# Head of a pairwise outer-product batch norm: order of loads, of the shift and of the gram terms, and which tiles start from raw products

## The chip, the cores and the metric

The kernel runs on one core of one Trainium2 chip. The metric is the device time of one execution in microseconds (us); lower is better. Times are medians of the fast runs; a profile is one execution. The kernel before takes 1891.19 us (median of 6 runs, 1891.06 to 1891.61), so 1 us is 0.05%, and the runs of one kernel spread over about 0.5 us.

Engines: PE multiplies matrices, DVE is the vector engine, ACT the scalar engine, POOL is GpSimd, SP only issues DMAs.

## The reference, cut to what matters

```python
# xi, xj: (1024, 39, 16) f32, W: (1, 16, 16)
rows, cols = np.tril_indices(39, k=-1)                # 741 pairs
cross  = xj[:, rows, :, None] * xi[:, cols, None, :]  # (1024, 741, 16, 16)
mean   = cross.mean(axis=(0, 2, 3)); var = ((cross - mean) ** 2).mean(axis=(0, 2, 3))
out    = ((cross - mean) * rsqrt(var + 1e-5) * gamma + beta) * W
```

The output has 1024 x 741 x 256 floats, 777 MB. The statistics of all pairs need the whole batch, but they follow from sums over the inputs (6 MB) alone, through small matrix products (the "grams"). Nothing can be stored before they are there, so the kernel has a head without stores and then a long stretch of stores.

## The kernel before

A partition holds eight batch rows, here called samples. Work goes by tiles: one row `r` of the triangle (its `r` pairs) for two samples. Tiles 0 to 3 are row 19. A scaled tile is made in two steps: POOL scales xi by each pair's factor (`scale_xi`), ACT and POOL multiply by xj (`products`), and DVE adds the pair's offset and multiplies by W (`finish`, one instruction for each pair; POOL does 13% of the pairs). The first tiles are made from raw products while the statistics are still under way, and then need an affine step and a weighing.

```python
RAW = 2
...
raw0 = raw_products(0, nc.scalar, range(32))
raw1 = raw_products(1, nc.scalar, range(8))
...                                   # sums of sample 0 of xj and xi together, shift
for n in range(2 * NT // T):          # 8 steps: two samples of xj or of xi
    square(n)                         # ACT
    emit(raw0, 2)                     # ACT, two raw products of tile 0
    moments(n)                        # DVE, the sum of squares
    ...
    if n % 2 == 1:
        gram(n // 2 * T)              # PE, three terms for each of two samples
    if n in (1, 3):
        sums(n + 3, n + 5)            # DVE
        ...
emit(raw_products(1, nc.gpsimd, range(8, 32)), 24)
nc.scalar.copy(w_dve, w_sb)
emit(raw0, 8)
nc.scalar.copy(g1, ps_g[0][0:F, 0 : 2 * F + 1])
...                                   # small operations on 39 x 39 tables
apply(0)                              # table of row 19, all partitions
affine(0)                             # ACT and POOL: y * s + t, pair by pair
weigh(0)                              # DVE: y * W, with the stores
scale_xi(2)
affine(1)
weigh(1)
apply(2)
apply(1)
for n in range(1, len(tiles)):
    if n == 1:
        products(2)
        scale_xi(3)
        continue
    scale_xi(n + 2)
    finish(n)                         # DVE with the stores
    ...
    products(n + 1)
```

## Time and profile before

| | before |
|---|---|
| time | 1891.19 us |
| span of the profiled run | 1889.3 us |
| first store issued | 41.27 us |
| DMA in the long middle (160 to 1800 us) | full, 423 GB/s |
| DVE, ACT, POOL busy | 92%, 86%, 83% |

Read it as two stretches: a head, and a long stretch in which the DMA engines are full. A "hole" below is time between the first store and that long stretch in which the DMA engines have too little to move.

### The profile page before, as it was taken

To read this page: it belongs to the slowest core of one execution; us is meant where nothing else is said; L and a number is where in the kernel's file an instruction comes from. 1 tells how busy PE (TensorE), PEld (TensorE's weight loads), DVE (VectorE), ACT (ScalarE), POOL (GpSimd) and SP (SyncE) were. 2 spreads that over 40 slices of the span, in tenths; PEclk is the share of its full clock that TensorE was granted. 3 is DMA by queue.
4 is the path that set the end of the run, shared out by engine and by line. 5 is a ranking of instruction groups with operands and counts; after the bars stand their busy time and mean duration, and the time that the engine had idled before them with its cause. 6 is when DMAs were issued, how large, how long until landed. Compare 5 with 4: busy or idle time off the path is not lost. (4 is left out here: it accounts for less than half of the span.)

```text
span 1889.3 us, 10288 instructions
## 1 busy us (share of the span) xinstructions
PE 24.5 (1%) x128; PEld 23.1 (1%) x128; DVE 1730.7 (92%) x2612; ACT 1621.3 (86%) x3625; POOL 1574.5 (83%) x1985
## 2 busy tenths in 40 slices
PE   3100000000000000000000000000000000000000
PEld 3100000000000000000000000000000000000000
DVE  7999999998989898989898989899999999999996
ACT  8999989898989898989898989888888888888762
POOL 9798878788888888888888888888888888888972
DMA  4999999999999999999999999999999999999999
GB/s 164 390 418 429 425 427 429 430 424 429 424 425 426 424 424 426 422 425 425 424 425 423 426 423 426 422 422 422 421 421 422 418 415 419 416 419 419 415 419 390
DMA packets 70288, 783.67 MB, mean 415 GB/s; under 512 B 5057, under 2 KB 6209, under 8 KB 15937
## 3 DMA queue, kind: packets, MB, share of 16 engines
q1 hardware_dynamic: 69632, 780.46, 98.3%
q10 hardware_dynamic: 576, 2.56, 0.3%
q14 instruction: 79, 0.64, 0.1%
q8 instruction: 1, 0.02, 0.0%
HBM read 6.00 MB, written 776.99 MB: 414 GB/s over the span
## 5 line engine op out<-in xcount | busy, mean ns | idle before, releaser
L238 DVE SCALAR_TENSOR_TENSOR y_sb<-y_sb,st_sb,w_dve 128x512 f32<-128x512 f32 x2542 | 1678.5, 740 | 131.5 <-issue 128.3
L139 ACT ACTIVATE y_sb<-xs,xj_sb 128x256 f32<-128x256 f32 (+32 forms) x3544 | 1576.4, 539 | 223.5 <-DMA out_dram<-y_sb 171.8
L141 POOL TENSOR_SCALAR y_sb<-xs,xj_sb 128x560 f32<-128x560 f32 (+35 forms) x1256 | 643.2, 536 | 35.1 <-DMA out_dram<-y_sb 32.6
L230 POOL TENSOR_TENSOR y_sb<-y_sb,w_sb 128x1024 f32<-128x1024 f32 (+4 forms) x138 | 442.0, 3203 | 11.5
L159 POOL TENSOR_TENSOR xs<-xi_sb,st_sb 128x576 f32<-128x576 f32 (+37 forms) x150 | 187.8, 1252 | 225.3 <-ACT y_sb L139 217.8
L226 POOL TENSOR_SCALAR y_sb<-y_sb,st_sb 128x512 f32<-128x512 f32 x384 | 259.4, 692 | 12.9 <-ACT y_sb L139 12.9
L204 DVE TENSOR_TENSOR y_sb<-y_sb,w_dve 128x2560 f32<-128x2560 f32 (+5 forms) x8 | 21.0, 2682 | 2.3 <-ACT y_sb L194 2.3
L139 ACT ACTIVATE y_sb<-xi_sb,xj_sb 128x304 f32<-128x304 f32 x40 | 18.7, 534 | 0.1
L414 PE MATMUL ps<-y_sb 39*128 39x38 f32 (+37 forms) x76 | 16.5, 397 | 5.6 <-DVE y_sb L402 5.6
L414 PEld LDWEIGHTS ps<-y_sb 39*128 39x128 f32 x76 | 16.3, 329 | 5.8 <-issue 5.8
L194 ACT ACTIVATE y_sb<-y_sb,st_sb 128x512 f32<-128x512 f32 x20 | 14.2, 797 | 0.0
L196 POOL TENSOR_SCALAR y_sb<-y_sb,st_sb 128x512 f32<-128x512 f32 x18 | 13.5, 771 | 0.3 <-issue 0.3
L141 POOL TENSOR_SCALAR y_sb<-xi_sb,xj_sb 128x304 f32<-128x304 f32 x24 | 11.9, 518 | 0.0
L299 DVE TENSOR_REDUCE y_sb<-y_sb 128x78 f32<-128x1248 f32 x8 | 11.1, 1442 | 0.0
L277 DVE TENSOR_REDUCE y_sb<-xj_sb 128x78 f32<-128x1248 f32 (+1 forms) x5 | 5.9, 1189 | 5.6 <-DMA xj_sb<-in_r_xj_dram 5.6
L293 ACT ACTIVATE y_sb<-y_sb 128x1248 f32<-128x1248 f32 x8 | 9.9, 1243 | 1.3 <-POOL y_sb L283 1.1
L283 POOL TENSOR_TENSOR y_sb<-xj_sb,y_sb 128x1248 f32<-128x1248 f32 x4 | 9.3, 2314 | 1.9 <-ACT y_sb L327 1.9
L283 POOL TENSOR_TENSOR y_sb<-xi_sb,y_sb 128x1248 f32<-128x1248 f32 x4 | 9.3, 2318 | 0.0
L316 PE MATMUL ps<-y_sb 128*39 128x79 f32 x48 | 7.2, 339 | 16.5 <-DVE y_sb L299 16.5
L316 PEld LDWEIGHTS ps<-y_sb 128*39 128x39 f32 x48 | 6.1, 183 | 17.4 <-DVE y_sb L299 9.6
L277 DVE TENSOR_REDUCE y_sb<-xi_sb 128x78 f32<-128x1248 f32 (+1 forms) x5 | 5.9, 1186 | 0.0
L259 POOL TENSOR_SCALAR_AFFINE_SELECT y_sb<-y_sb 39x4992 f32<-39x4992 f32 x1 | 4.6, 4623 | 0.0
(45 smaller groups left out, 16.9 us busy)
## 6 DMA issues: line engine op xcount, KB each, us to landing
out_dram<-y_sb SPq DMA_DIRECT2D x32, 3072.0 KB, 13.7
out_dram<-y_sb SPq DMA_DIRECT2D x28, 2816.0 KB, 15.7
out_dram<-y_sb SPq DMA_DIRECT2D x32, 1664.0 KB, 14.2
out_dram<-y_sb SPq DMA_DIRECT2D x16, 3328.0 KB, 17.2
out_dram<-y_sb SPq DMA_DIRECT2D x30, 1536.0 KB, 15.2
out_dram<-y_sb SPq DMA_DIRECT2D x12, 3840.0 KB, 17.6
out_dram<-y_sb SPq DMA_DIRECT2D x12, 3584.0 KB, 18.1
out_dram<-y_sb SPq DMA_DIRECT2D x22, 1792.0 KB, 17.4
```

What stands on the lines that cost most here:

```text
L139: nc.scalar.activation(y, src, AF.Copy, scale=scale)
L141: engine.tensor_scalar(y, src, scale, 1.0, ALU.mult, ALU.mult)
L159: nc.gpsimd.tensor_tensor(xs, xi_sb[:, t0 : t0 + T, 0:r, :], s_sb[:, :, n0 : n0 + r, :].to_broadcast([P, T, r, E]), ALU.mult,)
L194: nc.scalar.activation(y[:, :, c, :], y[:, :, c, :], AF.Identity, bias=t_c, scale=s_c)
L196: nc.gpsimd.tensor_scalar(y[:, :, c, :], y[:, :, c, :], s_c, t_c, ALU.mult, ALU.add)
L204: nc.vector.tensor_tensor(y[:, :, c0:c1, :], y[:, :, c0:c1, :], w_dve.unsqueeze(1).to_broadcast([P, T, c1 - c0, EE]), ALU.mult,)
L226: nc.gpsimd.tensor_scalar(y[:, :, c, :], y[:, :, c, :], t_sb[:, n0 + c : n0 + c + 1], 1.0, ALU.add, ALU.mult)
L230: nc.gpsimd.tensor_tensor(y[:, :, split:r, :], y[:, :, split:r, :], w_sb.unsqueeze(1).to_broadcast([P, T, r - split, EE]), ALU.mult,)
L238: stt(y[:, :, c, :], y[:, :, c, :], t_sb[:, n0 + c : n0 + c + 1], w_dve.to_broadcast([P, T, EE]), ALU.add, ALU.mult,)
L283: nc.gpsimd.tensor_tensor(devs[n % 7], sources[x][:, t0 : t0 + T], shift[:, x : x + 1, :].unsqueeze(3).to_broadcast([P, T, F, E]), ALU.sub ...
L316: nc.tensor.matmul(acc[0:F, 0 : 2 * F + 1], lhs, fb[:, t], start=t == 0, stop=t == NT - 1)
L414: nc.tensor.matmul(ps[:, :, first[r] - n0 : first[r] - n0 + r], pick[:, r, :], stq[:, :, 0:r], start=True, stop=True,)
```

## The change

The intent is a shorter head: the first sample of xi arrives first and alone, so that its shift is known sooner and POOL can begin; the gram terms are issued as soon as their inputs are there, so that the table operations run beside the last matmuls; only tile 0 is made raw, and tile 1 takes the ordinary route but is finished sample by sample, so that its stores can begin when half of it is there.

```diff
-    (0, 2, 5, 9, 14, 19), (0, 6, 12, 19), ...
+    (0, 2, 5, 9, 14, 19), (0, 4, 9, 14, 19), ...
-POOL_I, POOL_I_LONG = 4, 5
+POOL_I, POOL_I_LONG, POOL_I_FIRST = 4, 5, 6      # tiles 1 and 2: POOL has 6 of 16 products
-LOADS = (0, 1, 2, 4, 8)
+LOADS = (1, 2, 3, 4, 8)
-    RAW = 2
+    RAW = 1
@@ finish
+        size = 1 if n == RAW else T
+        for t in range(0, T, size):
+            for c0, c1 in zip(bounds(n), bounds(n)[1:]):
+                for c in range(c0, min(c1, split)):
+                    stt(y[:, t : t + size, c, :], ...)
+                store(n, c0, c1, t, t + size)
@@ loads
+        nc.sync.dma_start(xi_sb[:, 0, 0 : F // 2], xi_v[:, 0, 0 : F // 2])
+        nc.scalar.dma_start(xi_sb[:, 0, F // 2 : F], xi_v[:, 0, F // 2 : F])
+        nc.sync.dma_start(xj_sb[:, 0], xj_v[:, 0])
@@ statistics: xi first in every step
-            t0, x = n // 2 * T, n % 2
+            return n // 2 * T, 1 - n % 2
+        def gram(n):
+            ...
+                terms = ((0, fa[:, t, 0:F]), (2, ones[:, 0:F])) if x else ((1, fa[:, t, F : 2 * F]),)
             moments(n)
+            gram(n)
-            if n in (1, 3):
-                sums(n + 3, n + 5)
+            if n == 1:
+                sums(4, 8)
@@ tables
-        nc.scalar.activation(p_kk, k, AF.Square)
+        nc.vector.tensor_mul(p_kk, k, k)
...
@@ first tiles
         apply(0)
-        affine(0)
+        apply(1)
+        affine(0, range(0, 11))
+        scale_xi(1)
+        affine(0, range(11, mid))
         weigh(0)
+        products(1)
         scale_xi(2)
-        affine(1)
-        weigh(1)
-        apply(2)
-        apply(1)
```

(Cut: the shift's copies, the order of the small operations, the row groups of the tables; eight raw products of tile 0 that go from ACT to POOL; ACT's first square root, which loads its table and now stands before ACT's last load.)

More of the change, by code (lines that the diff above doesn't have):

```diff
@@ L19 @@
 FIRST_PIECES = (
-    (0, 2, 5, 9, 14, 19), (0, 6, 12, 19), (0, 4, 11, 19), (0, 9, 19), (0, 10, 20), (0, 9, 18), (0, 10, 20), (0, 9, 18)
+    (0, 2, 5, 9, 14, 19), (0, 4, 9, 14, 19), (0, 4, 11, 19), (0, 9, 19), (0, 10, 20), (0, 9, 18), (0, 10, 20), (0, 9, 18)
 )
-POOL_I, POOL_I_LONG = 4, 5
+POOL_I, POOL_I_LONG, POOL_I_FIRST = 4, 5, 6
 POOL_SHARE = 0.13
-LOADS = (0, 1, 2, 4, 8)
+LOADS = (1, 2, 3, 4, 8)
 ROW_GROUPS = (
-    (19, 20, 0, None), (15, 19, 1, None), (20, 25, 1, None), (1, 15, 2, 8), (25, 32, 3, 16), (32, 39, 4, 24)
+    (19, 20, 0, None), (15, 19, 1, None), (20, 25, 2, 1), (1, 15, 2, 8), (25, 32, 3, 16), (32, 39, 4, 24)
 )
@@ L169, in products @@
         xs = xs_of.pop(n)
-        split = E - (POOL_I_LONG if tiles[n][0] > TWO else POOL_I)
+        split = E - (POOL_I_FIRST if n < 3 else POOL_I_LONG if tiles[n][0] > TWO else POOL_I)
         for t in range(T):
@@ L173, in products, with store @@
                 product(n, nc.scalar if i < split else nc.gpsimd, t, i, xs[:, t])
-    def store(n, c0, c1):
+    def store(n, c0, c1, t_from=0, t_to=T):
         r, t0, _ = tiles[n]
         n0 = first[r]
-        step = 1 if r > ONE and c1 == r else T
-        for t in range(0, T, step):
+        step = 1 if r > ONE and c1 == r else t_to - t_from
+        for t in range(t_from, t_to, step):
             nc.sync.dma_start(
@@ L184, in store, with affine @@
             )
-    def affine(n):
+    def affine(n, pairs):
         r = tiles[n][0]
         y = view(n)
-        for c in range(r):
+        for c in pairs:
             s_c = st_sb[:, 0, first[r] + c : first[r] + c + 1]
@@ L235, in finish @@
             )
-        for c0, c1 in zip(bounds(n), bounds(n)[1:]):
-            for c in range(c0, min(c1, split)):
-                stt(
-                    y[:, :, c, :],
-                    y[:, :, c, :],
-                    t_sb[:, n0 + c : n0 + c + 1],
-                    w_dve.to_broadcast([P, T, EE]),
-                    ALU.add,
-                    ALU.mult,
-                )
-            store(n, c0, c1)
+        size = 1 if n == RAW else T
+        for t in range(0, T, size):
+            for c0, c1 in zip(bounds(n), bounds(n)[1:]):
+                for c in range(c0, min(c1, split)):
+                    stt(
+                        y[:, t : t + size, c, :],
+                        y[:, t : t + size, c, :],
+                        t_sb[:, n0 + c : n0 + c + 1],
+                        w_dve.to_broadcast([P, size, EE]),
+                        ALU.add,
+                        ALU.mult,
+                    )
+                store(n, c0, c1, t, t + size)
     with tc.manual_schedule():
+        nc.gpsimd.memset(ones, 1.0)
+        nc.sync.dma_start(xi_sb[:, 0, 0 : F // 2], xi_v[:, 0, 0 : F // 2])
+        nc.scalar.dma_start(xi_sb[:, 0, F // 2 : F], xi_v[:, 0, F // 2 : F])
+        nc.sync.dma_start(xj_sb[:, 0], xj_v[:, 0])
         for t0, t1 in zip(LOADS, LOADS[1:]):
+            if t1 == NT:
+                nc.scalar.activation(shift_r, ones[0:F, 0:1], AF.Sqrt)
             nc.sync.dma_start(xj_sb[:, t0:t1], xj_v[:, t0:t1])
@@ L255, in tile_pair_outer_batchnorm @@
         nc.sync.dma_start(w_sb[:, 0, :], w.rearrange("o i j -> (o i j)").partition_broadcast(P))
-        nc.gpsimd.memset(ones, 1.0)
         nc.gpsimd.memset(fb[:, :, 2 * F : 2 * F + 1], 1.0 / NB)
@@ L273, in part, with sums @@
             return slice(x * F, (x + 1) * F)
-        def sums(t0, t1):
-            for x in range(2):
+        def sums(t0, t1, xs=(1, 0)):
+            for x in xs:
                 nc.vector.tensor_reduce(
@@ L279, in sums, with step_of @@
                 )
+        def step_of(n):
+            return n // 2 * T, 1 - n % 2
         def deviation(n):
-            t0, x = n // 2 * T, n % 2
+            t0, x = step_of(n)
             nc.gpsimd.tensor_tensor(
@@ L290, in square @@
         def square(n):
-            scale = 0.25 / NB**0.5 if n % 2 else 0.25
+            _, x = step_of(n)
+            scale = 0.25 / NB**0.5 if x else 0.25
             nc.scalar.activation(devs[n % 7], devs[n % 7], AF.Square, scale=scale)
         def moments(n):
-            t0, x = n // 2 * T, n % 2
+            t0, x = step_of(n)
             to = fb if x else fa
-            at = slice(F, 2 * F)
-            nc.vector.tensor_reduce(to[:, t0 : t0 + T, at], devs[n % 7], AX.X, ALU.add)
-        def means(n):
-            t0, x = n // 2 * T, n % 2
-            to = fb if x else fa
-            stt(
-                to[:, t0 : t0 + T, 0:F],
-                total[:, t0 : t0 + T, part(x)],
-                1.0 / (E * NB) if x else 1.0 / E,
-                ps_u[:, x : x + 1, :].to_broadcast([P, T, F]),
-                ALU.mult,
-                ALU.subtract,
-            )
@@ L313, in gram, with means @@
-        def gram(t0):
+            nc.vector.tensor_reduce(
+                to[:, t0 : t0 + T, F : 2 * F], devs[n % 7], AX.X, ALU.add
+            )
+        def means(t0, t1):
+            for x, to in enumerate((fa, fb)):
+                stt(
+                    to[:, t0:t1, 0:F],
+                    total[:, t0:t1, part(x)],
+                    1.0 / (E * NB) if x else 1.0 / E,
+                    ps_u[:, x : x + 1, :].to_broadcast([P, t1 - t0, F]),
+                    ALU.mult,
+                    ALU.subtract,
+                )
@@ L314, in gram @@
+        def gram(n):
+            t0, x = step_of(n)
             for t in range(t0, t0 + T):
-                for acc, lhs in zip(ps_g, (fa[:, t, 0:F], fa[:, t, F : 2 * F], ones[:, 0:F])):
+                terms = ((0, fa[:, t, 0:F]), (2, ones[:, 0:F])) if x else ((1, fa[:, t, F : 2 * F]),)
+                for acc, lhs in terms:
                     nc.tensor.matmul(
-                        acc[0:F, 0 : 2 * F + 1], lhs, fb[:, t], start=t == 0, stop=t == NT - 1
+                        ps_g[acc][0:F, 0 : 2 * F + 1], lhs, fb[:, t], start=t == 0, stop=t == NT - 1
@@ L318, in gram @@
                     )
-        raw0 = raw_products(0, nc.scalar, range(32))
-        raw1 = raw_products(1, nc.scalar, range(8))
-        nc.scalar.activation(shift_r, ones[0:F, 0:1], AF.Sqrt)
-        sums(0, 1)
-        nc.tensor.matmul(ps_s[:, 0 : 2 * F], ones, total[:, 0], start=True, stop=True)
-        nc.tensor.matmul(ps_c[0:F, 0:1], total[:, 0, 0:F], ones[:, 0:1], start=True, stop=True)
-        nc.scalar.activation(
-            shift.rearrange("p x f -> p (x f)"), ps_s[:, 0 : 2 * F], AF.Copy, scale=k_s
-        )
+        raw0 = raw_products(0, nc.scalar, range(24))
@@ new lines, in tile_pair_outer_batchnorm @@
+        raw0_pool = raw_products(0, nc.gpsimd, range(24, 32))
+        ps_shift = (ps_g[0][:, 0:F], ps_s[:, 0:F])
+        for x in (1, 0):
+            sums(0, 1, (x,))
+            nc.tensor.matmul(ps_shift[x], ones, total[:, 0, part(x)], start=True, stop=True)
+        nc.tensor.matmul(ps_c[0:F, 0:1], total[:, 0, 0:F], ones[:, 0:1], start=True, stop=True)
+        ps_u = ps_s[:, 2 * F : 4 * F].rearrange("p (x f) -> p x f", x=2)
+        nc.scalar.activation(shift[:, 1], ps_shift[1], AF.Copy, scale=k_s)
@@ L330, in tile_pair_outer_batchnorm @@
+        nc.scalar.activation(ps_u[:, 1], shift[:, 1], AF.Copy, scale=1.0 / NB)
+        nc.scalar.activation(shift[:, 0], ps_shift[0], AF.Copy, scale=k_s)
+        nc.scalar.copy(ps_u[:, 0], shift[:, 0])
         nc.scalar.activation(shift_r, ps_c[0:F, 0:1], AF.Copy, scale=k_s)
-        ps_u = ps_s[:, 2 * F : 4 * F].rearrange("p (x f) -> p x f", x=2)
-        nc.scalar.copy(ps_u[:, 0], shift[:, 0])
-        nc.scalar.activation(ps_u[:, 1], shift[:, 1], AF.Copy, scale=1.0 / NB)
         def cell(n):
@@ L343, in tile_pair_outer_batchnorm @@
         sums(1, 2)
-        means(0)
-        means(1)
-        sums(2, 4)
-        means(2)
-        means(3)
+        means(0, 2)
+        sums(2, 3)
+        sums(3, 4)
+        means(2, 4)
         for n in range(7):
@@ L355, in tile_pair_outer_batchnorm @@
             moments(n)
+            gram(n)
             if n == 0:
                 deviation(7)
-            if n % 2 == 1:
-                gram(n // 2 * T)
-            if n in (1, 3):
-                sums(n + 3, n + 5)
-                means(n + 3)
-                means(n + 4)
-        emit(raw_products(1, nc.gpsimd, range(8, 32)), 24)
+            if n == 1:
+                sums(4, 8)
+                means(4, 8)
+        emit(raw0_pool, 8)
         nc.scalar.copy(w_dve, w_sb)
-        emit(raw0, 8)
         nc.scalar.copy(g1, ps_g[0][0:F, 0 : 2 * F + 1])
+        emit(raw0, 1)
         nc.scalar.copy(e_aa, ps_g[1][0:F, 2 * F : 2 * F + 1])
-        emit(raw0, 5)
+        emit(raw0, 4)
         e_ab, e_abb, e_a = g1[:, 0:F], g1[:, F : 2 * F], g1[:, 2 * F : 2 * F + 1]
@@ L380, in tile_pair_outer_batchnorm @@
         stt(k, p_b, u, e_ab, ALU.mult, ALU.add)
-        stt(q2, e_ab, u, p_aab, ALU.mult, ALU.add)
+        stt(p_q1, p_bb, u, e_abb, ALU.mult, ALU.add)
         stt(k, p_v, e_a, k, ALU.mult, ALU.add)
-        stt(q2, p_v_half, e_aa, q2, ALU.mult, ALU.add)
-        stt(p_q1, p_bb, u, e_abb, ALU.mult, ALU.add)
-        stt(p_q2, q2, 2.0, p_v, ALU.mult, ALU.mult)
         nc.vector.tensor_add(q1, p_q1, e_abb)
         stt(p_mean, p_v, u, k, ALU.mult, ALU.add)
-        nc.scalar.activation(p_kk, k, AF.Square)
+        nc.vector.tensor_mul(p_kk, k, k)
+        stt(q2, e_ab, u, p_aab, ALU.mult, ALU.add)
         stt(q1, q1, u, p_aabb, ALU.mult, ALU.add)
+        stt(q2, p_v_half, e_aa, q2, ALU.mult, ALU.add)
+        nc.vector.tensor_sub(q1, q1, p_kk)
+        stt(p_q2, q2, 2.0, p_v, ALU.mult, ALU.mult)
         nc.vector.tensor_add(q1, q1, p_q2)
-        nc.vector.tensor_sub(q1, q1, p_kk)
         nc.vector.tensor_scalar(p_var, q1, 0.0, BN_EPS, ALU.max, ALU.add)
@@ L396, in tile_pair_outer_batchnorm @@
         nc.scalar.activation(rstd, inv, AF.Sqrt)
-        emit(raw1, 8)
         nc.vector.tensor_mul(p_newton, p_var, rstd)
@@ L429, in tile_pair_outer_batchnorm @@
         apply(0)
-        affine(0)
+        apply(1)
+        affine(0, range(0, 11))
+        scale_xi(1)
+        affine(0, range(11, mid))
         weigh(0)
+        products(1)
         scale_xi(2)
-        affine(1)
-        weigh(1)
-        apply(2)
-        apply(1)
         for n in range(1, len(tiles)):
-            if n == 1:
-                products(2)
-                scale_xi(3)
-                continue
             if n + 2 < len(tiles):
```

## The prediction

> **What bounds the kernel now.** I read the busy table by stretches first, then the order of instructions in the first 90 us, then the list of waits. The split of the span at 41.27 us (the first store is issued), 82 and 160 us gives this; the columns that matter are the DVE, ACT and POOL busy times, then at the end the share of the DMA engines and GB/s.
>
> ```profile
> core 0: us, PE busy (x) PEld busy (x) DVE busy (x) ACT busy (x) POOL busy (x), PEclk, DMA share, GB/s
> 0.00:41.27 41.27, 12.58 (x74) 11.33 (x74) 28.87 (x48) 33.00 (x65) 38.38 (x44) 1.00 0.37 146
> 41.27:82.00 40.73, 11.95 (x56) 11.74 (x56) 39.02 (x41) 40.73 (x84) 32.92 (x46) 1.00 0.91 368
> 82.00:160.00 78.00, 0.00 (x0) 0.00 (x0) 77.97 (x121) 78.00 (x180) 71.19 (x93) 1.00 1.00 420
> 160.00:1800.00 1640.00, 0.00 (x0) 0.00 (x0) 1516.33 (x2301) 1434.03 (x3252) 1387.87 (x1767) 1.00 1.00 423
> ```
>
> From 82 us on the DMA engines are full and stay full: 777 MB must go out at about 423 GB/s, and nothing in the change touches that. What can move is when the stores start and how many holes the DMA has before 82 us. Slices of 1 us show the last hole at 81 to 82 us (share 0.61), larger ones at 70 to 72 us (0.33, 0.00). So up to 82 us the stores wait for the engines, and the end of the kernel moves by as much as the first store of the fourth tile (tile 3) moves. The order of instructions up to there (start, duration, engine, line; x is a count of merged ones):
>
> ```profile
> 4.93 0.80 DVE L277 TENSOR_REDUCE y_sb<-xj_sb 128x39 f32<-128x624 f32 x1 [4.93 <-DMA xj_sb<-in_r_xj_dram]
> 7.63 2.31 POOL L283 TENSOR_TENSOR y_sb<-xj_sb,y_sb 128x1248 f32<-128x1248 f32 x1 [1.93 <-ACT y_sb L327]
> 23.83 5.52 DVE L299 TENSOR_REDUCE y_sb<-y_sb 128x78 f32<-128x1248 f32 x4
> ...
> 31.77 0.20 ACT L372 COPY y_sb<-ps 39x79 f32<-39x79 f32 x1
> 32.00 0.25 DVE L380 SCALAR_TENSOR_TENSOR y_sb<-ps,y_sb 39x39 f32<-39x39 f32 x1 [2.65 <-ACT y_sb L372]
> 36.42 0.19 DVE L402 SCALAR_TENSOR_TENSOR y_sb<-ps,y_sb 39x39 f32<-39x39 f32 x1
> 37.41 0.18 DVE L425 TENSOR_TENSOR ps<-ps,st_sb 128x19 f32<-128x19 f32 x1 [0.80 <-PE ps L414]
> 39.13 14.20 ACT L194 ACTIVATE y_sb<-y_sb,st_sb 128x512 f32<-128x512 f32 x20
> 40.03 1.22 DVE L204 TENSOR_TENSOR y_sb<-y_sb,w_dve 128x1024 f32<-128x1024 f32 x1 [2.13 <-ACT y_sb L194]
> 41.27 45.59 SPq L181 DMA_DIRECT2D out_dram<-y_sb  x13
> 41.44 19.74 DVE L204 TENSOR_TENSOR y_sb<-y_sb,w_dve 128x1536 f32<-128x1536 f32 x7 [0.19 <-ACT y_sb L194]
> 53.23 37.13 ACT L139 ACTIVATE y_sb<-xs,xj_sb 128x304 f32<-128x304 f32 x84
> 63.96 26.42 DVE L238 SCALAR_TENSOR_TENSOR y_sb<-y_sb,st_sb,w_dve 128x512 f32<-128x512 f32 x40 [1.44 <-ACT y_sb L139]
> ```
>
> Three milestones: M, the last sum of squares on DVE ends, 29.35; S, the table of the first row group is ready (37.73 plus 0.17), 37.90; D, DVE begins to finish tile 2, 63.96. From D on DVE runs without a pause, and tile 3's first nine pairs are ready 26 steps of 0.659 us later (17 pairs of tile 2, nine of tile 3), at 81.1: the hole just named. So the gain is the shift of D.
>
> **What the Trainium skill says.** "VectorE: DVE Perf Modes", section on the TRN2 errata: a fixed cost per instruction, not a factor, so halved operands cost more than half. The trace agrees: a 512-element finishing step starts every 0.659 us, and where one waited it resumed in parts of 0.128 and 0.531 (512/0.96 GHz is 0.533). I take 0.128 + 256/960 = 0.395 us for a 256-element step. "DMA: Bandwidth & Descriptors", Queues, rings and completion order: each DMA engine takes turns between the queue rows; so loads of the two queues share the rate[...]. Here xj's and xi's first samples, issued together, landed at 4.91 and 5.07. "ScalarE: Activation LUTs", What ACT_TABLE_LOAD costs: about 1283 ns; the trace has 1.28 at 3.15, hidden behind the loads before and after.
>
> **The change, part by part.**
> *Loads and sums.* xi's first sample alone, half on each queue, is 0.32 MB ahead of the first sum instead of 0.64. At the 0.42 MB/us of the early slices that is 0.76 us; I take the first sum at 4.2 instead of 4.93. But DVE, not POOL, bounds the statistics: it works 23.45 of the 24.47 us from 4.93 to 29.40, while POOL's last deviation ends at 25.87. Its work hardly changes: eight one-sample sums at 0.725, two four-sample sums at 2.66, eight sums of squares at 1.36, six means at 0.15 to 0.23, together 23.0. What changes is its waiting. Sharing the rate as before, I expect about 0.4 us for xj's first sample, 0.3 for samples two and three, 0.3 for the second square, and 0.85 for xi's samples 4 to 7, which landed at 15.99 and would land near 15.1 (0.16 MB fewer on that queue) when DVE is free at 14.25. M = 4.2 + 23.0 + 1.85 = 29.05: 0.3 earlier.
> *M to S.* Before 8.55 us: 2.65 until DVE starts (six terms on PE, then ACT's copy held by raw products until 31.77), 2.80 to the reciprocal, 1.81 to the last table term, 1.48 to S. Now the grams that g1 needs are done after the last-but-one sum, so DVE starts about 0.1 after M; thirteen small operations at about 0.23 make 3.0; ACT's square becomes a DVE product and ACT is free for the root. 0.1 + 3.0 + 1.81 + 1.48 = 6.4, less 0.1 for the better spacing of dependent operations: 6.3. S = 35.3, that is 2.6 earlier.
> *S to D.* Before 26.06 us. ACT lost 1.1 us by eight raw products running to 39.13, but tile 1 was already multiplied out. Now tile 1 takes the full route. POOL: nine affines at 0.747, one scaling of 1.21, twelve products at 0.492 (6 of 16, two samples) bring it to S + 14.0; a scaling, S + 15.2; the next scaling needs a buffer that ACT reads until S + 0.1 + 10 x 0.71 + 20 x 0.442 = S + 16.1, so it ends at S + 17.4; two adds and a product with w (1.45 + 2.33), S + 21.2; twelve products of tile 2 (5.90), S + 27.1. ACT has tile 2's at S + 24.9. DVE: the second row group holds it until about S + 1.85 (four rows more on PE at 0.427, three small operations), tile 0's weighing takes 10.5, tile 1's 34 half steps 13.4, the third row group 0.8: S + 26.6. The last of the three is POOL: D = S + 27.1, 1.0 later after S than before. D = 62.4.
> *Stores.* First store at S + 1.85 + 1.14 = 38.3, 3.0 earlier. Tile 1's first sample can't be complete before POOL's S + 21.2 = 56.5, and the stores go out in order, so I expect a hole of about 1 us there, and larger ones than now near tile 2's first two pieces. They eat the rest of the 3.0.
>
> Sum: 0.3 (M) + 2.3 (M to S) - 1.0 (S to D) = 1.6 us; with my doubt that the load waits are all that large I say 1.75.
>
> **Rivals.** (1) The earlier first store counts in full: gain 3.0, 1888.3. For it: the stream is DMA-bound for 95% of the span. Against: the holes at 70 to 72 and 81 us are set by DVE and POOL. (2) POOL and ACT cannot give tile 1 in time: if the half steps cost 0.45 instead of 0.395, DVE ends at S + 28.5, and with load waits as large as mine the gain is nothing, 1891. For it: POOL is the busiest engine of the head and gets tile 1's products on top. (3) The loads sample by sample remove DVE's waits altogether: M near 27.5 and a gain of 3.3, 1888. Against: before, the last pair of loads landed at 15.02 and 15.99, and the bytes are the same.
>
> **Range and chances.** 1891.26 - 1.75 = 1889.5. M is uncertain by about 0.6, M to S by 0.3, S to D by 0.8; together about 1.1 us for one side, a little wider for the store holes: 1887.9 to 1890.9. Two per cent is 38 us, nearly the whole head of 41 us, so within 2% is all but certain.
>
> **What would show it.** M at 28.5 to 29.4, with a wait of DVE for xi's load near 14 us; the first small operation within 0.3 us of M; S near 35.3; the first store near 38.3; D near 62.4, released by POOL's products; a hole in the DMA near 56 us and one near 80 us. If there is no hole near 80 us, the stores themselves bound the stretch and rival 1's reasoning is the right one; if D is released by DVE's half steps, it is rival 2. A DMA rate in the long middle other than 423 GB/s would make the prediction wrong without any of these.

## The result, and the profile after

The changed kernel takes 1889.91 us (median of 6 runs, 1889.49 to 1890.09) against 1891.19 of the same rounds: 1.28 us less. The ratio is 0.9992, 95% interval 0.998 to 1.0005. (Ratios are the mean time of one kernel's fast runs over that of the other's of the same rounds, so not quite the ratio of the medians quoted.) The predicted time was 1889.5, the range 1887.9 to 1890.9; the measured time lies within it. The six times of one kernel and the six of the other do not overlap, so the 1.28 us are clear of the noise, small as they are.

The busy times of the changed kernel by stretches, cut at its first store, 80 and 160 us (columns as in the same view of before):

```profile
0.00:38.33 38.33, 13.68 (x74) 11.22 (x74) 29.36 (x51) 26.70 (x50) 30.09 (x27) 1.00 0.40 157
38.33:80.00 41.67, 12.32 (x58) 12.11 (x57) 40.73 (x68) 41.67 (x92) 40.36 (x59) 1.00 0.89 359
80.00:160.00 80.00, 0.00 (x0) 0.00 (x0) 79.97 (x125) 80.00 (x183) 74.00 (x94) 1.00 1.00 418
160.00:1800.00 1640.00, 0.00 (x0) 0.00 (x0) 1516.64 (x2301) 1431.73 (x3246) 1386.34 (x1764) 1.00 1.00 423
```

The long middle is the same, 423 GB/s. The stores begin 2.9 us earlier, but the stretch after them has more holes (share 0.89). The order of instructions of the changed kernel, with the lines that answer to those of before:

```profile
3.90 0.80 DVE L286 TENSOR_REDUCE y_sb<-xi_sb 128x39 f32<-128x624 f32 x1 [3.90 <-DMA xi_sb<-in_r_xi_dram]
...
6.08 2.32 POOL L296 TENSOR_TENSOR y_sb<-xi_sb,y_sb 128x1248 f32<-128x1248 f32 x1 [0.37 <-ACT y_sb L345]
...
15.57 2.75 DVE L286 TENSOR_REDUCE y_sb<-xi_sb 128x156 f32<-128x2496 f32 x1 [1.56 <-DMA xi_sb<-in_r_xi_dram]
...
21.48 8.24 DVE L312 TENSOR_REDUCE y_sb<-y_sb 128x78 f32<-128x1248 f32 x6
...
29.81 0.25 DVE L392 SCALAR_TENSOR_TENSOR y_sb<-ps,y_sb 39x39 f32<-39x39 f32 x1
...
35.16 0.17 DVE L438 TENSOR_TENSOR st_sb<-ps,st_sb 128x19 f32<-128x19 f32 x1
...
37.09 10.55 DVE L204 TENSOR_TENSOR y_sb<-y_sb,w_dve 128x1024 f32<-128x1024 f32 x5
38.33 31.95 SPq L181 DMA_DIRECT2D out_dram<-y_sb  x15
...
47.56 13.40 DVE L241 SCALAR_TENSOR_TENSOR y_sb<-y_sb,st_sb,w_dve 128x256 f32<-128x256 f32 x34
...
56.55 5.95 POOL L141 TENSOR_SCALAR y_sb<-xs,xj_sb 128x304 f32<-128x304 f32 x12
...
62.54 7.99 DVE L241 SCALAR_TENSOR_TENSOR y_sb<-y_sb,st_sb,w_dve 128x512 f32<-128x512 f32 x12 [0.90 <-POOL y_sb L141]
```

M, the end of the six sums of squares, is 21.48 + 8.24 = 29.72, later than before (29.35), although the first sum starts 1.03 us earlier and POOL 1.55 us earlier; DVE stood for 1.56 us before the sums of samples 4 to 7. The first small operation follows M at once, and S is 35.16 + 0.17 = 35.33 (37.90 before). D is 62.54 (63.96 before), released by POOL's products: 1.42 us earlier, nearly the change in time.

To see where the gain settles, I added up the bytes of the DMA records from 30 us on (a few instruction fetches among them; with the stores' queue alone the last column moves by up to 0.14 us) and noted when 5, 38, ... pairs of two samples (0.262 MB each) had been written:

| pairs written (tile) | before, us | after, us | after less before |
|---|---|---|---|
| 5 (0) | 46.17 | 42.98 | -3.20 |
| 38 (end of 1) | 67.57 | 65.17 | -2.39 |
| 42 (first store of 2) | 70.36 | 68.92 | -1.43 |
| 57 (end of 2) | 81.70 | 80.29 | -1.41 |
| 152 (end of 7) | 141.53 | 140.10 | -1.43 |
| 1500 | 971.98 | 970.74 | -1.24 |

The lead of 3.2 us shrinks to 1.4 at the first store of tile 2, the one that D releases, and stays there to the end. One-microsecond slices of the changed kernel show three of the holes that eat it (the last two columns are the DMA share and GB/s; a smaller one is at 56 us, share 0.74):

```profile
65.00:66.00 1.00, 0.00 (x0) 0.00 (x0) 1.00 (x3) 1.00 (x4) 0.92 (x2) 1.00 0.08 31
69.00:70.00 1.00, 0.00 (x0) 0.00 (x0) 1.00 (x3) 1.00 (x3) 1.00 (x3) 1.00 0.00 0
80.00:81.00 1.00, 0.00 (x0) 0.00 (x0) 1.00 (x3) 1.00 (x3) 0.69 (x2) 1.00 0.42 172
```

### The profile page after: what moved, and what is told of

Same layout as the page of the kernel before. It is cut to its first block, busy times and chain, and to the rows that moved or that the text cites. A ratio compares the mean times of both kernels' runs of the same rounds, so it can differ in the third digit from the quotient of the medians.

```text
span 1887.8 us, 10327 instructions
## 1 busy us (share of the span) xinstructions
PE 26.0 (1%) x130; PEld 23.3 (1%) x130; DVE 1733.7 (92%) x2642; ACT 1614.1 (86%) x3615; POOL 1574.9 (83%) x1980
## 2 busy tenths in 40 slices
DMA packets 71056, 783.68 MB, mean 415 GB/s; under 512 B 5184, under 2 KB 6592, under 8 KB 16704
## 5 line engine op out<-in xcount | busy, mean ns | idle before, releaser
L241 DVE SCALAR_TENSOR_TENSOR y_sb<-y_sb,st_sb,w_dve 128x512 f32<-128x512 f32 (+1 forms) x2576 | 1692.1, 738 | 130.7 <-issue 128.0
L139 ACT ACTIVATE y_sb<-xs,xj_sb 128x320 f32<-128x320 f32 (+32 forms) x3560 | 1583.2, 537 | 225.8 <-DMA out_dram<-y_sb 180.4
L141 POOL TENSOR_SCALAR y_sb<-xs,xj_sb 128x512 f32<-128x512 f32 (+34 forms) x1272 | 652.5, 540 | 37.9 <-DVE y_sb L241 22.0
L230 POOL TENSOR_TENSOR y_sb<-y_sb,w_sb 128x512 f32<-128x512 f32 (+4 forms) x139 | 444.4, 3197 | 11.6
L159 POOL TENSOR_TENSOR xs<-xi_sb,st_sb 128x640 f32<-128x640 f32 (+37 forms) x151 | 189.2, 1253 | 215.2 <-ACT y_sb L139 209.0
L139 ACT ACTIVATE y_sb<-xi_sb,xj_sb 128x304 f32<-128x304 f32 x24 | 11.6, 534 | 0.0
L286 DVE TENSOR_REDUCE y_sb<-xi_sb 128x39 f32<-128x624 f32 (+1 forms) x5 | 5.9, 1187 | 5.5 <-DMA xi_sb<-in_r_xi_dram 5.5
L204 DVE TENSOR_TENSOR y_sb<-y_sb,w_dve 128x2560 f32<-128x2560 f32 (+3 forms) x5 | 10.5, 2175 | 0.0
L194 ACT ACTIVATE y_sb<-y_sb,st_sb 128x512 f32<-128x512 f32 x10 | 7.2, 800 | 2.6 <-DVE st_sb L438 2.6
L141 POOL TENSOR_SCALAR y_sb<-xi_sb,xj_sb 128x304 f32<-128x304 f32 x8 | 4.0, 524 | 0.0
## 6 DMA issues: line engine op xcount, KB each, us to landing
out_dram<-y_sb SPq DMA_DIRECT2D x32, 3072.0 KB, 13.6
```

What stands on the lines that cost most here:

```text
L139: nc.scalar.activation(y, src, AF.Copy, scale=scale)
L141: engine.tensor_scalar(y, src, scale, 1.0, ALU.mult, ALU.mult)
L159: nc.gpsimd.tensor_tensor(xs, xi_sb[:, t0 : t0 + T, 0:r, :], s_sb[:, :, n0 : n0 + r, :].to_broadcast([P, T, r, E]), ALU.mult,)
L204: nc.vector.tensor_tensor(y[:, :, c0:c1, :], y[:, :, c0:c1, :], w_dve.unsqueeze(1).to_broadcast([P, T, c1 - c0, EE]), ALU.mult,)
L230: nc.gpsimd.tensor_tensor(y[:, :, split:r, :], y[:, :, split:r, :], w_sb.unsqueeze(1).to_broadcast([P, T, r - split, EE]), ALU.mult,)
L241: stt(y[:, t : t + size, c, :], y[:, t : t + size, c, :], t_sb[:, n0 + c : n0 + c + 1], w_dve.to_broadcast([P, size, EE]), ALU.add, ALU.mult,)
```

## The experiments

Twelve kernels ran, each with five timed rounds; all were correct. I compare "time less before"; the changed kernel has -1.28 us. Theory A is that of the prediction: the time moves with D. Theory C is its rival 1: the time moves with the first store.

| run | S | first store | D | D less before | time | before | time less before |
|---|---|---|---|---|---|---|---|
| changed kernel | 35.33 | 38.33 | 62.54 | -1.42 | 1889.91 | 1891.19 | -1.28 |
| e1_old_loads | 36.34 | 39.35 | 63.55 | -0.41 | 1890.55 | 1891.08 | -0.53 |
| e2_whole_tile | 35.33 | 38.33 | 63.41 | -0.55 | 1890.78 | 1891.08 | -0.30 |
| e4_late_store | 35.41 | 40.74 | 62.60 | -1.36 | 1890.05 | 1891.08 | -1.03 |
| e5_cut_tile3 | 35.72 | 38.73 | 62.93 | -1.03 | 1889.92 | 1891.08 | -1.16 |
| e3_sums_later | 34.20 | 37.21 | 61.40 | -2.56 | 1888.51 | 1891.25 | -2.74 |
| e6_old_grams | 37.32 | 40.32 | 64.52 | +0.56 | 1891.46 | 1891.25 | +0.21 |
| e7_two_raw | 38.88 | 43.34 | 64.29 | +0.33 | 1891.23 | 1891.25 | -0.02 |
| e8_cut_all | 35.33 | 38.34 | 62.54 | -1.42 | 1889.98 | 1891.25 | -1.27 |
| e9_two_raw_act | 35.36 | 39.81 | 60.75 | -3.21 | 1887.72 | 1891.14 | -3.42 |
| e10_cut_on | 35.49 | 38.50 | 62.74 | -1.22 | 1903.45 | 1891.14 | +12.31 |
| e11_two_raw_cut | 35.66 | 40.11 | 61.05 | -2.91 | 1902.61 | 1891.14 | +11.47 |
| e12_sums_cut | 34.40 | 37.40 | 61.63 | -2.33 | 1902.31 | 1891.14 | +11.17 |

The calls ran on different chips, and the kernel before came out at 1891.08 to 1891.25 there. In all rows but the last three, "time less before" follows "D less before" within 0.35 us, over a range of 3.8 us, while the first store moves by 6 us without such a relation. That is the main evidence for theory A. D in this table is one profiled execution, and the head itself varies: the kernels that share the changed kernel's loads and statistics (the changed one, e2, e4, e5, e8, e10) had M at 29.72, 29.72, 29.80, 30.12, 29.73 and 29.89.

### e1: the loads of before

```diff
-LOADS = (1, 2, 3, 4, 8)
+LOADS = (0, 1, 2, 4, 8)
-        nc.sync.dma_start(xi_sb[:, 0, 0 : F // 2], ...)    # and the two lines after it
```

> The changed kernel with the loads of before (xj and xi whole samples 0, 1, 2 to 3, 4 to 7; nothing cut). Theory A (the end moves with D, the start of DVE's work on tile 2): DVE waits for xi's samples 2 and 3, which landed at 10.7 us before, so M, the end of the last sum of squares, moves from 29.72 to about 30.5, S and D follow by the same 0.8, and the time is 0.8 us longer than the changed kernel's (about 1890.7). Theory B (cutting the loads cost more than it gave, since DVE waited 1.56 us for xi's samples 4 to 7): M near 29.3 and the time about 0.4 us shorter (1889.5).

```profile
22.50 8.24 DVE L309 TENSOR_REDUCE y_sb<-y_sb 128x78 f32<-128x1248 f32 x6
```

M came at 22.50 + 8.24 = 30.74, D at 63.55, the time is 0.75 us longer than the changed kernel's (-0.53 against -1.28). Theory A holds and theory B falls: cutting the loads gained about 1.0 us at M, given the order of the sums. So M is late for another reason than the cut.

### e2: tile 1 not finished by samples

```diff
-        size = 1 if n == RAW else T
+        size = T
```

> The changed kernel with tile 1 finished in steps of both samples (512 elements) instead of sample by sample. S stays at 35.3. DVE can't start on tile 1 before ACT has its last product (near 51.4); 17 steps of 0.659 and the third row group follow, so D moves from 62.5 to about 63.7. Theory A: the time is 1.2 us longer (about 1891.1). Theory C (the end moves with the first store, which stays at 38.3): unchanged, 1889.9.

```profile
51.54 11.28 DVE L241 SCALAR_TENSOR_TENSOR y_sb<-y_sb,st_sb,w_dve 128x512 f32<-128x512 f32 x17 [3.92 <-ACT y_sb L139]
...
63.41 11.93 DVE L241 SCALAR_TENSOR_TENSOR y_sb<-y_sb,st_sb,w_dve 128x512 f32<-128x512 f32 x18
```

DVE waits 3.92 us for ACT's last product and then works in large steps; D is 0.87 us later and the time 0.98 us longer, with the first store unmoved at 38.33. Finishing by samples is worth about 0.9 us, although its 34 half steps (one pair of one sample, 256 elements) took 13.40 us (0.394 each) where 17 whole ones take 11.28.

### e4: a later first store

```diff
-    (0, 2, 5, 9, 14, 19), (0, 4, 9, 14, 19), ...
+    (0, 5, 9, 14, 19), (0, 4, 9, 14, 19), ...
```

> The changed kernel with tile 0's first two pieces joined: the first store covers five pairs and is issued near 40.5 instead of 38.3 us; DVE's later work keeps its time, D stays near 62.5. Theory A: the DMA has 2 us less lead, but the holes at 56, 65, 69 and 80 us swallow it, time unchanged (1889.9, within 0.3). Theory C: 2.0 us longer (1891.9).

```profile
40.74 25.11 SPq L181 DMA_DIRECT2D out_dram<-y_sb  x13
62.60 4.04 DVE L241 SCALAR_TENSOR_TENSOR y_sb<-y_sb,st_sb,w_dve 128x512 f32<-128x512 f32 x6 [0.23 <-POOL y_sb L141]
```

The first store came 2.41 us later (40.74), D stayed (62.60), and the time grew by 0.25 us, less than the spread of this kernel's own runs (0.42). Theory C, the first store, would have had it grow by the whole 2.4. The first store by itself is worth next to nothing here.

### e5 and e8: finer stores near the last hole

```diff
 # e5
-(0, 4, 11, 19), (0, 9, 19), ...
+(0, 4, 11, 19), (0, 4, 9, 19), ...
 # e8
-(0, 4, 11, 19), (0, 9, 19), (0, 10, 20), ...
+(0, 2, 5, 9, 14, 19), (0, 4, 9, 14, 19), (0, 5, 10, 20), ...
```

> The changed kernel with tile 3's first store (nine pairs) cut into four and five pairs, nothing else. D stays at 62.5. Theory A, completed: what sets the end is the last hole in the DMA, at 80 to 81 us, 0.6 us wide; with four pairs ready 3.3 us earlier it closes, and the time is 0.5 us shorter (about 1889.4). Theory A as I wrote it (D alone) or theory C (the first store): unchanged.

> The changed kernel with the stores of tiles 2, 3 and 4 cut finer: (0, 2, 5, 9, 14, 19), (0, 4, 9, 14, 19), (0, 5, 10, 20). D stays at 62.5. The run with tile 3 alone cut was not faster: its DMA had gained 0.4 us at tile 3 and gave it back at tile 4's first store of ten pairs, so the bound is DVE's work plus the size of the piece that is waited for, through tile 4. With all of them cut the DMA follows DVE by one small piece: I work out 76 pairs written near 90.6 instead of 92.7 and the time 2.0 us shorter, about 1887.9. Rival (the smaller stores lower the DMA's rate, or D alone counts whatever the pieces): within 0.4 us of 1889.9.

Neither is faster. In e5 the hole at tile 3 closed: 66 pairs were written at 86.48, as early as in the changed kernel (86.52), though this execution's D was 0.39 later. But at 96 pairs it was again later by 0.32, just D's lateness. In e8 the DMA led the changed kernel by 1.46 us at 66 pairs and by 1.09 at 152, and by nothing (0.01) at 200. Where it went is one hole, in one-microsecond slices of e8:

```profile
138.00:139.00 1.00, 0.00 (x0) 0.00 (x0) 1.00 (x3) 1.00 (x4) 1.00 (x1) 1.00 0.76 313
139.00:140.00 1.00, 0.00 (x0) 0.00 (x0) 0.97 (x3) 1.00 (x3) 1.00 (x2) 1.00 0.11 45
```

and in the same slice of the changed kernel:

```profile
139.00:140.00 1.00, 0.00 (x0) 0.00 (x0) 0.97 (x3) 1.00 (x3) 1.00 (x2) 1.00 0.92 378
```

From tile 8 on these tiles are stored whole. Both kernels issue the store at 139.80 us, when DVE has finished the whole tile; the changed kernel's DMA ran dry at just that time (152 pairs at 140.10), e8's a us before. So "the last hole, at 80 us" was not the last bound. DVE works without a pause from D to about 139 us, and the DMA stays within a store of it all the way: D alone counts, as the prediction concluded, but for a wider reason than it gave.

### e3: the late sums after one more sum of squares

```diff
-            if n == 1:
+            if n == 2:
                 sums(4, 8)
```

> The changed kernel with the sums of samples 4 to 7 put after the third sum of squares instead of after the second. In the changed kernel DVE stands idle for 1.56 us before them, waiting for xi's load; now one sum of squares (1.36 us, its input is ready at 14.3) fills that wait. Theory A: M moves from 29.7 to about 28.4, S and D follow (34.0, 61.2), the time is 1.2 us shorter than the changed kernel's, about 1888.7. Rival (POOL or ACT, not DVE, would then bound the statistics): POOL's last deviation ends at 24.7 whatever DVE does, and M comes no earlier than 27.4, so it could hold back no more than what is left below that; under it M would stay near 29.7 and the time at 1889.9.

```profile
11.56 4.33 DVE L312 TENSOR_REDUCE y_sb<-y_sb 128x78 f32<-128x1248 f32 x3
...
15.82 2.74 DVE L286 TENSOR_REDUCE y_sb<-xi_sb 128x156 f32<-128x2496 f32 x1
...
21.72 6.88 DVE L312 TENSOR_REDUCE y_sb<-y_sb 128x78 f32<-128x1248 f32 x5
```

The wait is filled with work: three sums of squares run up to the point where the load is there, and M is 21.72 + 6.88 = 28.60, 1.12 earlier than in the changed kernel. D is 1.14 earlier and the time 1.46 us shorter. DVE did bound the statistics, and 1.12 of the 1.56 us for which it stood idle in the changed kernel could be had by reordering.

### e6: the gram terms as before

```diff
-                terms = ((0, fa[:, t, 0:F]), (2, ones[:, 0:F])) if x else ((1, ...),)
+                terms = enumerate((fa[:, t, 0:F], fa[:, t, F : 2 * F], ones[:, 0:F]))
-            gram(n)
+            if n % 2 == 1:
+                gram(n)
```

> The changed kernel with the gram matmuls issued as before, all six terms of two samples after each second sum of squares. DVE can then start the small operations only when the last six terms (1.8 us on PE) and the copy are done: first small operation about 2.1 us after M instead of 0.1. Theory A: S, D and the time move by that, less nothing: S 37.1 to 37.3, D 64.3 to 64.5, time 1.8 to 2.0 us longer than the changed kernel's (about 1891.8). Rival (the table terms were not what held S): unchanged, 1889.9.

```profile
31.19 0.22 ACT L384 COPY y_sb<-ps 39x79 f32<-39x79 f32 x1 [3.64 <-PE ps L332]
...
31.80 0.25 DVE L393 SCALAR_TENSOR_TENSOR y_sb<-ps,y_sb 39x39 f32<-39x39 f32 x1 [1.71 <-PE ps L332]
```

DVE stands 1.71 us for PE. M to S is 37.32 - 30.09 = 7.23 instead of 5.61, D is 64.52, and the time is 1.49 us longer than the changed kernel's. The profiled run's M was itself 0.37 late, so D overstates it. This part of the change is worth about 1.5 us, more than the whole measured gain.

### e7 and e9: two raw tiles in the new head

```diff
-    RAW = 1
+    RAW = 2                      # raw0: all on ACT; raw1: 8 products on ACT, 24 on POOL;
+                                 # affine and weigh for tile 1, its stores as before (0, 6, 12, 19)
 ...
 # e9 besides:
-        nc.vector.tensor_mul(p_kk, k, k)
+        nc.scalar.activation(p_kk, k, AF.Square)     # and four raw products on ACT go behind it
```

> The changed kernel with raw products for tiles 0 and 1 as before (24 of tile 1 on POOL, 8 on ACT, tile 1 through affine and weighing), and tile 2's products shared 10 to 6 between ACT and POOL as in the changed kernel. It undoes the part about the first tile only. S unchanged, 35.3. ACT reaches the affines near S + 2.4, POOL near S + 1.2; the first store is later, S + 4.4 = 39.7. ACT: 20 affines of 0.71, 20 products of 0.442: D = S + 25.5 = 60.8 instead of 62.5. Theory A: the time is 1.3 to 1.7 us shorter, about 1888.4. Theory C (the first store counts, and making tile 1 scaled gains): 1.4 us longer, 1891.3.

D came at 64.29, not 60.8, and the time at -0.02. S to D was 64.29 - 38.88 = 25.41, as worked out (25.5); it was S that failed:

```profile
30.87 0.26 DVE L397 SCALAR_TENSOR_TENSOR ps<-ps,y_sb 39x39 f32<-39x39 f32 x1
31.05 3.54 DVE L398 TENSOR_TENSOR ps<-y_sb 39x39 f32<-39x39 f32 x1
34.51 0.24 DVE L399 SCALAR_TENSOR_TENSOR y_sb<-y_sb,ps 39x39 f32<-39x39 f32 x1
```

The product k x k, 0.19 us in the changed kernel, took 3.54 us. It is the only one of these small operations whose two tensor operands both lie in SBUF, and POOL was streaming raw products at the time (until 36.86); in the changed kernel POOL is idle there, from 28.73 to 35.58. The Trainium skill, "SBUF — State Buffer", section SBUF: two separate sides, says that a DVE operation with two SBUF inputs and a GpSimd operation that reads SBUF exclude each other. The trace fits that: 3.54 us beside the stream, 0.19 without it. e9 gives the square back to ACT, as before the change:

> The kernel with two raw tiles again, with the square of k made by ACT instead of a DVE product of two SBUF operands. In the first try that product stood on DVE for 3.54 us beside POOL's stream of raw products, and S came at 38.9 instead of 35.3; S to D was 25.4 us, as worked out (25.5). If that product alone was the cause, S is near 35.5, D near 61.0 (ACT's products then set it) and, by theory A, the time 1.4 us shorter than the changed kernel's: about 1888.5. Rival (two raw tiles cost M to S otherwise, by POOL's or ACT's load): S stays above 37 and the time at 1890 or more.

```profile
30.75 0.20 ACT L397 ACTIVATE ps<-y_sb 39x39 f32<-39x39 f32 x1
...
37.66 14.19 ACT L194 ACTIVATE y_sb<-y_sb,st_sb 128x512 f32<-128x512 f32 x20
...
60.75 14.57 DVE L241 SCALAR_TENSOR_TENSOR y_sb<-y_sb,st_sb,w_dve 128x512 f32<-128x512 f32 x22 [0.36 <-ACT y_sb L139]
```

S is back at 35.36 with the same raw products on POOL, so the stall was that one instruction; that the page's lock is the reason is not shown further than this. ACT reaches the affines 2.3 us after S, the first store is 1.48 us later than the changed kernel's, and yet D is 60.75 and the time 1887.72: 3.42 us less than before (ratio 0.9982, 0.997 to 0.9995) and 2.1 less than the changed kernel. In this head, "raw products for the first tile only" therefore costs time: it buys an early first store with a late D. e9 beats both kernels, and is the best that ran.

### e10, e11, e12: finer stores all the way

```diff
-        pieces = 1 + (r > ONE) + (r > TWO)
+        pieces = 1 + (r > 3) + (r > TWO)      # tiles of 4 to 24 pairs in two stores
```

e10 is e8 with this, e11 is e9 with this and e8's cuts, e12 is e3 with both.

> The changed kernel with the finer stores of tiles 2 to 4 and, from tile 8 on, tiles of 4 to 24 rows in two stores instead of one. With tiles 2 to 4 alone the DMA was 1.1 us ahead up to 152 pairs and lost it in a hole at 138 to 140 us, before the first store of a whole tile. If that switch to whole tiles is what gave the lead back, the lead stays: 1.1 us shorter than the changed kernel, about 1888.8. Rival (the lead is lost anyway, to buffers that are not free in time or to the cost of more stores): within 0.3 us of 1889.9.

> Two raw tiles with ACT's square, and the finer stores throughout. D near 61.0 leaves the DMA with work from the first store on (39.9): I expect no hole in the DMA between 45 and 160 us, so the first store sets the end, the other regime. The changed kernel loses some 4.7 us in holes after its first store and starts 1.6 us earlier: about 3 us shorter, 1886.5 to 1887. If the bound stays with D: 1.5 us for D and 1.1 for the cuts, 1887.3.

> The changed kernel with the later sums (1.4 us shorter alone) and the finer stores throughout. The two act on different terms, D and the lag of the DMA behind D, so they add: 1.4 + 1.1 = 2.5 us shorter than the changed kernel, about 1887.4. If the finer stores alone gave nothing in the end, 1888.5.

All three lost 11 to 12 us against before. The lead was there at first, as expected: at 200 pairs e10 was 1.08 us ahead of the changed kernel, e11 1.66, e12 2.23, and e11 had no slice with a DMA share under 0.8 between 43 and 165 us. It then melted at a steady rate. Two stretches of e10:

```profile
200.00:300.00 100.00, 0.00 (x0) 0.00 (x0) 98.21 (x152) 88.42 (x200) 82.86 (x105) 1.00 1.01 421
500.00:600.00 100.00, 0.00 (x0) 0.00 (x0) 93.00 (x141) 91.60 (x212) 84.57 (x105) 1.00 1.01 421
```

and of the changed kernel:

```profile
200.00:300.00 100.00, 0.00 (x0) 0.00 (x0) 94.39 (x145) 91.33 (x209) 84.47 (x111) 1.00 1.01 428
500.00:600.00 100.00, 0.00 (x0) 0.00 (x0) 93.40 (x143) 91.29 (x210) 84.34 (x108) 1.00 1.00 425
```

The DMA engines are full in both, but move 421 instead of 425 to 428 GB/s. Over the 1400 us from 200 to 1600 us, 1% is 14 us. e10 has 93,089 DMA packets, 39,760 of them under 8 KB, where the changed kernel has 71,056 and 16,704. From 1600 us on, where hardly a tile of 4 to 24 pairs is left, the rates are alike (417 and 416). That halving those stores costs the rate is shown by the step from e8 to e10, whose only edit it is. The packet records say how: between 200 and 1600 us a store packet of 4 KB took 163.8 ns on average in the changed kernel and one of 12 KB 467.2, so each costs about 12.1 ns beside 37.9 ns per KB; in e10 packets of these sizes took the same (163.6 and 467.8). e10 writes the same bytes in 84,736 store packets where e8 has 65,280, and 12.1 ns for each of the 19,456 more, shared by 16 engines, make 14.7 us (an estimate from these records) where 13.6 us were measured. No run varied the packets alone. My expectation had treated finer stores as free.

## Why the prediction was right or wrong

**The bound.** Right in what it concluded, incomplete in its ground. "The gain is the shift of D" holds within 0.35 us in ten kernels. The ground given, that the last hole is at 81 us, was too narrow: with that hole closed (e5, e8), the time stayed, since DVE holds the DMA at least until the store at 139.80 us.

**Loads and sums: wrong in sign.** The step that failed is "M = 4.2 + 23.0 + 1.85 = 29.05: 0.3 earlier"; M was 29.72, 0.37 later. The mis-sized term is the waiting of DVE. The first sum was earlier than I took it (3.90), but 29.72 - 3.90 - 23.0 leaves 2.8 us of waiting instead of 1.85. Of this, the wait before samples 4 to 7 was 1.56, where I had 0.85: xi's load, which the prediction had landing near 15.1, released DVE only at 15.57. The error was to let xi's load have the whole gain of a lighter queue. The last loads of xj and xi landed at 15.38 and 15.55, where they had landed at 15.02 and 15.99: one came as much earlier as the other came later. The DMA moved 407 to 477 GB/s in every us from 4 to 14, so the pair was there when all the bytes were through, and the bytes are the same. ACT also asked for its last load later, at 5.41 us instead of 2.2, behind the square root and its table load. That cost its queue at most the 0.66 us between its previous packet's end (8.30) and the first of this load (8.96), and the other queue used that time; asking earlier was not tried. e3 shows the waiting was avoidable, e1 that cutting the loads did not cause it.

**M to S: right in kind, too small.** Predicted 6.3, measured 5.61, before 8.55. DVE began 0.09 after M (0.1 predicted); the small operations took 2.42 us to the reciprocal where I had 3.0 from 0.23 each. The last ones before the reciprocal, each of which needs the one in front, start 0.22 to 0.23 us apart; most of the others start 0.11 to 0.17 apart. The sum has a slip too: its 1.81 ends with the last table term and its 1.48 begins with it (36.42 to 36.61), so its four parts make 8.74 and not 8.55, and 0.19 of the 0.69 us too many is this operation counted twice. e6 shows that the gram order carries 7.23 - 5.61 = 1.62 of the 2.94 us gained here; the rest (the order of the small operations, ACT freed of raw products) was not taken apart.

**S to D: right.** Predicted 27.1, measured 27.21, with POOL's products as the releaser, DVE ready 0.9 us and ACT 2.3 us before, and half steps of 0.394 us against 0.395. The 0.128 and 0.531 that the prediction reads as parts of a step that waited are not that: in the trace a semaphore instruction starts 0.128 us after a step, and the next step follows on time, 0.659 after the first. The fixed part holds all the same, since the two sizes give it: 2 x 0.394 - 0.659 = 0.129. The stretch is 1.15 us longer than before; against e9, which has two raw tiles in the same head (25.39), the single raw tile costs 1.82.

**The stores.** First store 38.33 (38.3 predicted); holes at 56, 65, 69 and 80 us, as foreseen. They ate 1.7 of the 2.9 us of lead.

**The sum.** 1.28 us instead of 1.75. Two errors of about 0.7 us, M too early and M to S too long, cancelled, so that S came out at 35.33 with 35.3 predicted by luck. The 0.15 us added to the sum of 1.6 for doubt about the load waits went the wrong way: they were larger.

**Rivals.** Rival 1 (the first store counts in full) fell with e4 and e9. Rival 2 (DVE's half steps bind) fell with the releaser of D. Rival 3 (no waits for loads, M near 27.5) did not happen, but e3 shows that 1.1 us of it was to be had without touching a load.

Open: e3 and e9 were not run together without the finer stores. In e9 ACT and POOL, busy with raw products, set the start of the affines, so their gains may not add.

## What to carry to other kernels

Before a DMA-bound stretch, look for the point up to which the stores still wait for the engines, and judge a head by when that point comes, not by when the first store goes out: here a first store 1.5 us later came with a time 2.1 us shorter. An engine that bounds the head must not stand before a load in program order while it has other ready work; moving one line gained more than the whole change. Cutting stores finer cost rate here where the DMA was full (421 GB/s instead of 425 to 428), so cut only where it is not.

## What the Trainium skill lacked or had wrong

- "SBUF — State Buffer", SBUF: two separate sides, has the loser of the shared pair blocked for the other's whole instruction. In e7 a DVE product of two SBUF operands took 3.54 us instead of 0.19, through seven GpSimd products that started every 0.49 us: one wait can last many instructions of a dense stream. The page doesn't say how the pair passes on.
- "DMA: Bandwidth & Descriptors", Rules for kernel authors, asks for at least 1 MiB in a DMA. In e10 339 of the 391 stores kept to that, and still the rate of the full DMA engines fell from 425 to 428 down to 421 GB/s: 13.6 us between e8 and e10. The rule does not say that stores above it still gain from being larger.
- No page that I used treats the lag between a producing engine and a full DMA queue in whole stores, which decided e5 and e8 (a lead of 1.1 us lost in one hole before a whole-tile store at 139.80 us).
